# Attention: GpSimd's addition tied to the minimum passes and first in its step, the root's power in two pieces, a third buffer of upper keys, small jobs paired

## The chip, the cores and the metric

The kernel runs on one core of a Trainium2 chip. The time is the device's time of one execution in microseconds; the median of three runs is given with the lowest and the highest. Five engines work side by side, each through its own queue and in the order of that queue: TensorE (PE; its weight loads are listed apart as PEld), VectorE (DVE), ScalarE (ACT), GpSimd (POOL) and SyncE (SP), which here only issues transfers. GpSimd also issues DMAs, among them transfers that add to their destination.

## The reference

A two-layer network on x of 2 x 256 x 64 x 64: an area attention, an LSTM-like recurrence, a Mamba-like convolution block and a mixture of experts, each behind a normalisation and added to its input. The change touches the first block alone:

```python
x = x + _L0_conv_ref(_ln_c(x), ...)
# _ln_c: over the 256 channels, (v - mean) / sqrt(var + 1e-6)
# _L0_conv_ref:
qk = _conv1x1_bn(x, w_qk, ...); vv = _conv1x1_bn(x, w_v, ...)
pp = _bn(depthwise 5x5 convolution of vv)
# 2 images x 4 areas of 1024 positions, 8 heads of 32 channels
attn = softmax(einsum('bhdn,bhdm->bhnm', q, k) * hd ** -0.5)
o = einsum('bhdm,bhnm->bhdn', v, attn)
return _conv1x1_bn(o + pp, w_proj, ...)
```

## The kernel before

**Tiling.** `area_attention` keeps all of x in SBUF, channels on partitions (two blocks c of 128). There are 8 areas of 1024 positions, and in each two groups of 4 heads (the two channel blocks): 16 groups G, called here the first (c = 0) and the second group of an area. A group has 16 steps t: n = t // 8 is the half of 512 queries, m = t % 8 the block of 128 keys. The loop runs over 256 steps.

**A step.** `scores` (L381, L386) makes two PSUM pairs of 2 x 512 scores for four heads, the row maxima (bf16 parts `mx`) being subtracted by a first small matmul; ScalarE takes two exponentials (L393) of them. `values` (L399) multiplies the exponentials of the step before with the transposed values. `maxima` (L286) works one group ahead, for the softmax's row maxima: in even steps with the key difference `kd` (upper minus lower keys), after which ScalarE rectifies both tiles (L298); in odd steps with the lower keys, after which VectorE runs four minimum passes (L302), one a head, that reduce to `nm`. Scores and maxima take four tiles a step from a pool of three pairs (`ps`, six PSUM banks); one more bank `po` serves all other matmuls, one after another, and `av_o` the values.

**Sums of exponentials.** The exponentials of four steps m, m+1, m+2, m+3 are added into the first one's tiles (`sx`, halves 0 and 1): by adding DMAs that GpSimd issues (L596, L602), and in the fourth step by one addition on GpSimd itself (L598), of the third step's half 1, which waits for the last matmul of that step's `maxima`. Three steps later `sums` multiplies them with ones; for the second half of the keys VectorE then runs a chain of five instructions (L425 to L433). In a first group's step 2 this chain belongs to the group before.

**Work for later, by hand.** All else is placed by tables: for each step t a list (offset, function, arguments). The offset counts groups in `BEFORE`, `BEHIND`, `LATE` and areas in `BEHIND_AREA`, `LATE_AREA` (a pair: first group, second group). BEFORE stands between `values` and `maxima`, BEHIND after them, LATE at the end of the step; taps stand ahead of BEHIND in even steps, and in odd steps behind it and `sums`; their number a step is in `TAPS`. The schedule is manual: every engine runs its instructions in the order in which this loop writes them. The functions are:

- next area's normalisation: `mean_sum` (VectorE), `mean_of_sum` (PE, copied by ScalarE), `centre` (VectorE, into the single buffer `xn`, which queries and keys of the area before read until the last query), `square` (ScalarE), `square_sum` (VectorE, L187), `variance_of_sum` (PE, ScalarE), `root` (DVE transpose, GpSimd's add and power, DVE transpose back), `scale` (VectorE);
- `query`, `key`, `v_half`: a projection of 512 columns (L160, four matmuls) that ScalarE evicts; `v_half` with half = 0 also copies border rows on GpSimd; `v_tokens`: four transposes (L249), copied by ScalarE;
- `join`, `place`: row maxima cut into three bf16 parts on GpSimd, turned by TensorE, copied by ScalarE (`rows`) and sent to `mx` by SyncE's DMAs;
- `key_difference` (VectorE, L274), late in step 15; the first matmuls of the next group's step 0 maxima read it;
- the area before: `add_taps`, `output` (L160, then L369 on VectorE), `shift` (ScalarE, L374).

**Taps.** The 5x5 convolution is 50 VectorE instructions an area (L345, L356), handed out by `TAPS`.

The first group has tables of its own (`..._FIRST`): it makes its own row maxima too, two `maxima` in each of its first eight steps.

Of the kernel before, what the change touches and what calls it, by code (L numbers as in the profile page):

```python
# [93 lines left out]
def area_attention(tc, sh, ap):  # L94
# [13 lines left out]
    with ExitStack() as ctx:  # L108
# [29 lines left out]
        early = [None]  # L138

# [17 lines left out]
        def project(wt, c, src, half, out):  # L157

            for k in range(2):
                nc.tensor.matmul(  # L160
                    out, wt[:, k, c * P : (c + 1) * P], src(k)[:, HALVES[half]], start=k == 0, stop=k == 1
                )
# [17 lines left out]
        def mean_sum(A):  # L180
            nc.vector.tensor_tensor(temp("pm", A), area(A)[:, 0], area(A)[:, 1], ALU.add)
# [4 lines left out]
        def square_sum(A):  # L186
            nc.vector.tensor_tensor(temp("sq0", A), temp("sq0", A), temp("sq1", A), ALU.add)  # L187
# [4 lines left out]
        def centre(A, c, at=FULL):  # L192
            if A not in xns:
                xns[A] = p1.tile([P, 2, NA], F32, name="xn")
            nc.vector.tensor_tensor(xns[A][:, c, at], area(A)[:, c, at], temp("pm", A)[:, at], ALU.subtract)
# [7 lines left out]
        def root(A, part, at=FULL):  # L203
            n = (at.stop - at.start) // 32
            if part == 0:
                turned = temp("ln_t", A)[:, at]
                nc.vector.transpose(turned, temp("var", A)[:, at])
                held["turned", at.start] = turned.rearrange("p (k i) -> p k i", i=32)[:, :, 0]
            elif part == 1:
                t = held.pop(("turned", at.start))  # L210
                y = held["root", at.start] = p1.tile([P, NA // 32], F32, name="root")[:, :n]
                nc.gpsimd.tensor_scalar(y, t, 1e-6, None, ALU.add)
                nc.gpsimd.tensor_tensor(y, y, minus_half.to_broadcast([P, n]), ALU.pow)
            else:
                y = held.pop(("root", at.start))
                nc.vector.transpose(
                    temp("ln_r", A)[:, at].rearrange("p (k i) -> p k i", i=32),
                    y.unsqueeze(2).to_broadcast([P, n, 32]),
                )

        def scale(A, c, at=FULL):
            nc.vector.tensor_tensor(xns[A][:, c, at], xns[A][:, c, at], temp("ln_r", A)[:, at], ALU.mult)
# [4 lines left out]
        def v_half(A, c, half):  # L227

            if A not in vhs:
                vhs[A] = p2.tile([P, 2, AROWS + 4, WW], F32, name="vh")  # L230
            ps, r0 = bank(), 2 + half * AROWS // NQ
            project(w["wv"], c, columns(xns[A]), half, ps)
            nc.scalar.activation(
                vhs[A][:, c, r0 : r0 + AROWS // NQ].rearrange("p r w -> p (r w)"), ps, AF.Identity,
                scale=s_v[:, c : c + 1], bias=t_v[:, c : c + 1],
            )
            if half == 0 and AREAS[A][1] > 0:
                nc.gpsimd.tensor_copy(vhs[A][:, c, 0:2], vhs[A - 1][:, c, AROWS : AROWS + 2])
                nc.gpsimd.tensor_copy(vhs[A - 1][:, c, AROWS + 2 :], vhs[A][:, c, 2:4])
# [12 lines left out]
        def rows_of(wt, G, half, name, s, t, ps):  # L252
            A, c = GROUPS[G]
            ps = bank() if ps is None else ps
            project(wt, c, columns(xns[A]), half, ps)
            out = p2.tile([P, 512], F32, name=f"{name}{half}")
            nc.scalar.activation(out, ps, AF.Identity, scale=s[:, c : c + 1], bias=t[:, c : c + 1])
            return out

        def query(G, half, ps=None):  # L260
            if half == 0:
                nms[G] = p2.tile([P, NQ, GH, NM], F32, name="nm")
            qs[G, half] = rows_of(w["wq"], G, half, "q", s_qk, t_qk, ps)

        def key(G, half, ps=None):
            ks[G, half] = rows_of(w["wk"], G, half, "k", s_qk[:, 2:4], t_qk[:, 2:4], ps)
# [4 lines left out]
        def key_difference(G):  # L271

            kds[G] = p1.tile([P, 512], F32, name="kd")
            nc.vector.tensor_tensor(kds[G], ks[G, 1], ks[G, 0], ALU.subtract)  # L274
# [5 lines left out]
        def maxima(G, at):  # L280

            i, n = CHUNKS[at] if G == 0 else divmod(at, 2)
            keys = ks[G, n] if G == 0 else ks[G, 0] if n else kds[G]
            tiles = [wide(), wide()]
            for h in range(GH):
                mm = nc.tensor.matmul(  # L286
                    tiles[h // 2][:, h % 2], qs[G, i // HM][head(h), i % HM * P : (i % HM + 1) * P],
                    keys[head(h)], start=True, stop=True, tile_position=(HD * h, 0),
                )
            if G == 0:  # L290
                for j in range(2):
                    nc.vector.tensor_reduce(  # L292
                        nms[G][:, n, 2 * j : 2 * j + 2, i], tiles[j], AX.X, ALU.max, negate=True
                    )
            elif n == 0:
                held["more"] = [p1.tile([P, 2, 512], F32, name=f"more{j}") for j in range(2)]
                for j in range(2):
                    nc.scalar.activation(held["more"][j], tiles[j], AF.Relu)  # L298
            else:
                for h in range(GH):  # L300
                    more = held["more"][h // 2][:, h % 2]
                    nc.vector.tensor_tensor_reduce(  # L302
                        more, tiles[h // 2][:, h % 2], more, -1.0, 3.0e38, ALU.add, ALU.min,
                        accum_out=nms[G][:, 0, h, i : i + 1],
                    )
            return mm.ins
# [15 lines left out]
        def place(G, half):  # L322
# [8 lines left out]
            mxs[G, half] = p2.tile([P, 512], BF16, name=f"mx{half}")  # L331
# [6 lines left out]
        def taps(A):  # L338

            vh, a = vhs[A], AREAS[A][1]  # L340
            for lower in range(2):
                for c in range(2):
                    if not lower:
                        acc = accs[A, c] = p1.tile([P, AROWS, WW], F32, name=f"acc{c}")
                        nc.vector.tensor_scalar(  # L345
                            acc, vh[:, c, 2 : 2 + AROWS], w_pe[:, c, 12:13], t_pe[:, c : c + 1], ALU.mult, ALU.add
                        )
                        yield
                    for k in range(25):
# [6 lines left out]
                        nc.vector.scalar_tensor_tensor(  # L356
                            part, vh[:, c, 2 + r0 + dy : 2 + r1 + dy, w0 + dx : w1 + dx],
                            w_pe[:, c, k : k + 1], part, ALU.mult, ALU.add,
                        )
                        yield  # L360

        def add_taps(A, c):
            y = ys[A, c]
            nc.vector.tensor_tensor(y, y, accs.pop((A, c)).rearrange("p r w -> p (r w)"), ALU.add)

        def output(A, co, half):
            ps, to = bank(), area(A)[:, co, HALVES[half]]
            project(w["wpr"], co, lambda k: ys[A, k], half, ps)
            nc.vector.scalar_tensor_tensor(to, ps, s_pr[:, co : co + 1], to, ALU.mult, ALU.add)  # L369
# [44 lines left out]
        def sums(G, n, half, exs):  # L414
# [18 lines left out]
            nc.vector.tensor_tensor(y, y, total, ALU.mult)  # L433
# [3 lines left out]
        with ExitStack() as own:  # L437
# [12 lines left out]
            def norm(at, half):  # L450
# [7 lines left out]
                root(0, 1, at)  # L458
                yield
                root(0, 2, at)  # L460
# [13 lines left out]
            query(0, 0, wide()[:, 0])  # L474
# [28 lines left out]
            for c in range(2):  # L503
# [8 lines left out]
        BEFORE = {3: [(0, place, 1)], 14: [(1, place, 0)]}  # L512
        BEHIND = [
            {0: [(1, query, 1)], 11: [(2, query, 0)], 13: [(2, key, 0)], 15: [(2, key, 1)]},
            {5: [(1, query, 1)], 9: [(2, query, 0)], 13: [(2, key, 0)], 15: [(2, key, 1)]},
# [3 lines left out]
                1: [(0, v_tokens, 0, 1), (-1, shift, 0)], 3: [(0, v_tokens, 1, 0), (1, square_sum)],  # L519
                4: [(1, variance_of_sum, 0)], 5: [(1, variance_of_sum, 1), (-1, shift, 1)], 7: [(-1, output, 0, 0)],  # L520
                8: [(-1, output, 0, 1)], 9: [(-1, output, 1, 0)], 12: [(0, v_tokens, 1, 1)],
            },
            {
                0: [(1, v_half, 0, 0)], 1: [(1, v_half, 1, 0)], 3: [(1, v_half, 0, 1), (2, mean_sum)],
                4: [(2, mean_of_sum, 0)], 7: [(-1, output, 1, 1)], 8: [(2, mean_of_sum, 1)],
                11: [(1, v_half, 1, 1)], 12: [(1, v_tokens, 0, 0)],
# [5 lines left out]
                0: [(1, centre, 0)], 1: [(1, centre, 1), (1, square, 0)], 2: [(1, square, 1)],  # L532
                4: [(-1, add_taps, 1)], 6: [(1, root, 0)], 7: [(1, root, 1)],
                9: [(1, root, 2), (1, scale, 0), (1, scale, 1)],
# [5 lines left out]
        BEHIND_FIRST = {**BEHIND[0], 0: [(1, key, 1)]}  # L540
# [6 lines left out]
        for t in range(16):  # L547
# [3 lines left out]
            [2, 0, 1, 1, 2, 2, 2, 1, 2, 0, 0, 2, 3, 2, 3, 0],  # L551
            [4, 1, 1, 1, 3, 2, 3, 2, 2, 1, 1, 2, 2, 1, 2, 0],
# [19 lines left out]
        for g in range(16 * len(GROUPS)):  # L572
# [14 lines left out]
            works(G, t, BEFORE_FIRST if new else BEFORE, {})  # L587

            mm = None
# [5 lines left out]
            if m % 4:  # L595
                nc.gpsimd.dma_start(total[0], exs[0], accum_op=ALU.add)  # L596
# [4 lines left out]
            if m % 2:  # L601
                nc.gpsimd.dma_start(total[1], exs[1], accum_op=ALU.add)  # L602
# [4 lines left out]
            works(G, t, BEHIND_FIRST if new else BEHIND[c], BEHIND_AREA[c])  # L607
# [1724 lines left out]
```

## Time and profile before

| What | us |
|---|---|
| median of 3 runs (lowest, highest) | 2896.4 (2896.26, 2899.74) |
| profiled execution, time | 2893.63 |
| profiled execution, span | 2891.8 |
| attention's loop, from the first score matmul (61.0) to the start of the last group (1293.0) | 1232 |
| areas 1 to 6 of it, 241.2 to 1212.8 | 971.6 |
| TensorE busy in these | 950.80 |
| VectorE, ScalarE, GpSimd busy in these | 836.36, 680.91, 459.06 |

A line of instructions by time reads: start, duration, engine, line, operation, out<-in, shapes, count, and in brackets the idle time of that engine before it and what ended it. A line by stretches reads: from:to, length, then busy time and number of instructions of TensorE, its weight loads, VectorE, ScalarE and GpSimd, the granted TensorE clock (1.00 is full), the mean busy share of the DMA engines and their GB/s. Some instructions of before:

| Instruction | mean ns |
|---|---|
| L393 exponential, L298 rectified maxima (128 x 1024) | 1029 |
| L302 minimum pass, and its read-out | 687, 83 |
| L274 key difference: lowest, median, highest of 15 | 685, 961, 3324 |
| L187 sum of squares: lowest, median, highest of 7 | 1398, 2240, 4094 |
| L598 GpSimd's addition (128 x 1024) | 2684 |
| L213 GpSimd's power, 32 columns; 16 columns | 6359; 2934 |
| L195 centring, L222 scale (128 x 1024) | 1226, 1222 |
| L198 square, L374 shift (128 x 1024) | 1066, 1152 |
| L257 eviction of a query or key, L421 and L412 copies (128 x 512) | 778, 593 |

### The profile page before, as it was taken

What the parts mean: (1) busy time and instruction counts of PE and PEld (TensorE: products, weight loads), DVE (VectorE), ACT (ScalarE), POOL (GpSimd) and SP (SyncE); (2) the same over time, 40 slices, a digit from 0 to 9 for tenths busy, and PEclk for the clock granted to TensorE, in tenths of its full rate; (3) what the DMA queues carried; (4) which work ended last, traced back from release to release, by engine and by line L of the source; (5) the groups of instructions that cost most, each with busy time, mean ns of one, the idle gap of its engine ahead of it and who ended that gap; (6) DMA issues with size and microseconds to landing.
All of it is one profiled execution on the core that took longest, in us unless ns stands there. A gap on an engine that the chain in (4) does not pass through costs nothing.

```text
span 2891.8 us, 45886 instructions
## 1 busy us (share of the span) xinstructions
PE 2631.5 (91%) x17234; PEld 1483.3 (51%) x17234; DVE 1963.8 (68%) x3729; ACT 1554.5 (54%) x2641; POOL 1239.8 (43%) x1164
## 2 busy tenths in 40 slices
PE   7899999999999999997799999878885699999984
PEld 2223333333333333321699999833443588888873
DVE  5788879898888979786566667788887522222116
ACT  3567676666767676763344555576645522222223
POOL 1444545444444445443221000078771266666651
PEclk9999999999999999998899999989998899999995
DMA  3566666666676666767240000035553266666648
GB/s 132 110 128 126 129 128 131 126 132 131 128 137 132 132 132 127 138 130 144 90 175 1 2 1 1 9 99 150 142 136 122 87 235 221 229 225 227 229 171 342
DMA packets 104826, 388.16 MB, mean 134 GB/s; under 512 B 19656, under 2 KB 20560, under 8 KB 94864
## 3 DMA queue, kind: packets, MB, share of 16 engines
q0 software_dynamic: 71488, 293.00, 43.0%
q1 hardware_dynamic: 31872, 87.86, 9.4%
q10 hardware_dynamic: 1232, 4.25, 0.4%
q8 instruction: 138, 2.26, 0.3%
q14 instruction: 96, 0.79, 0.1%
HBM read 173.30 MB, written 43.58 MB: 75 GB/s over the span
## 4 chain that ended last, share of the span: by engine, by line
PE 73%; DVE 11%; issue 5%; DMA 4%; ACT 3%; POOL 3%; SPq 0%; ACTq 0%; DVEq 0%; POOLq 0%
PE ps L286 9%; PE ph L2078 9%; PE py L2088 8%; PE po L160 7%; PE av_o L399 7%; PE z L805 7%; PE z L817 7%; PE ps L386 6%; DMA sx<-ex 3%; PE ps L381 3%; PE yp L1560 2%; PE po L399 2%; DVE hs L1550 2%; DVE more L302 1%; DVE acc L356 1%
## 5 line engine op out<-in xcount | busy, mean ns | idle before, releaser
L356 DVE SCALAR_TENSOR_TENSOR acc<-vh,w_pe,acc 128x1008 f32<-128x1008 f32 (+7 forms) x384 | 529.5, 1382 | 9.1
L596 POOL DMA_DIRECT2D sx<-ex x192 | 166.7, 868 | 692.7 <-DMA sx<-ex 278.3
L393 ACT ACTIVATE ex<-ps 128x1024 f32<-128x1024 f32 x384 | 376.1, 1029 | 125.9 <-PE ps L386 50.4
L302 DVE CUSTOM_DVE_ANT_0 more<-ps,more 128x512 f32<-128x512 f32 x480 | 302.9, 687 | 133.5 <-PE ps L286 124.6
L2080 ACT ACTIVATE act<-ph,wt 128x256 f32<-128x256 f32 x272 | 128.8, 474 | 386.5 <-PE ph L2078 379.1
L2068 DVE COPY xt<-px 128x512 f32<-128x512 f32 x68 | 47.0, 692 | 396.5 <-PE px L2066 396.5
L2078 PE MATMUL ph<-xt,wt 128*128 128x256 f32 x1088 | 291.6, 391 | 5.0 <-ACT act L2080 3.0
L386 PE MATMUL ps<-q,k 32*128 32x512 f32 x2048 | 285.2, 602 | 0.0
L2088 PE MATMUL py<-wt,act 128*128 128x256 f32 x1088 | 278.7, 379 | 0.0
L298 ACT ACTIVATE more<-ps 128x1024 f32<-128x1024 f32 x240 | 233.4, 1028 | 26.8 <-issue 9.1
L2078 PEld LDWEIGHTS ph<-xt,wt 128*128 128x128 f32 x1088 | 190.4, 191 | 68.0 <-DVE xt L2068 24.0
L805 PE MATMUL z<-xs,u 128*128 128x128 f32 x1872 | 224.0, 277 | 0.0
L805 PEld LDWEIGHTS z<-xs,u 128*128 128x128 f32 x1872 | 217.7, 194 | 0.2 <-issue 0.2
L829 ACT ACTIVATE t<-z,bias 128x128 f32<-128x128 f32 x468 | 136.3, 361 | 145.1 <-PE z L817 145.1
L399 PE MATMUL av_o<-ex,vt 128*32 128x512 f32 x1536 | 212.0, 613 | 2.4 <-ACT ex L393 2.4
L2088 PEld LDWEIGHTS py<-wt,act 128*128 128x128 f32 x1088 | 201.6, 190 | 24.7
L2103 POOL DMA_INDIRECT results<-y,ri x136 | 138.0, 1014 | 138.9 <-DVE y L2096 115.6
L286 PE MATMUL ps<-k,q 32*128 32x512 f32 x1088 | 182.6, 639 | 1.7 <-DVE nm L292 1.3
L817 PE MATMUL z<-xs,v 128*128 128x128 f32 x1512 | 180.0, 275 | 0.1
L817 PEld LDWEIGHTS z<-xs,v 128*128 128x128 f32 x1512 | 174.2, 192 | 0.7 <-DVE xs L836 0.7
L598 POOL TENSOR_TENSOR sx<-sx,ex 128x1024 f32<-128x1024 f32 x64 | 171.8, 2684 | 4.7 <-PE ps L286 4.7
L1557 POOL TENSOR_TENSOR cs<-hs,cs 128x1024 f32<-128x1024 f32 x63 | 149.0, 2367 | 55.4 <-DVE hs L1550 33.8
(435 smaller groups left out, 4607.8 us busy)
## 6 DMA issues: line engine op xcount, KB each, us to landing
sx<-ex POOLq DMA_DIRECT2D x320, 512.0 KB
cs<-c_rows SPq DMA_DIRECT2D x128, 256.0 KB
y<-results SPq DMA_DIRECT2D x32, 512.0 KB
x<-xrows SPq DMA_DIRECT2D x8, 1024.0 KB
rows<-xt SPq DMA_DIRECT2D x16, 512.0 KB
out_x<-res POOLq DMA_DIRECT2D x15, 512.0 KB
xrows<-xn SPq DMA_DIRECT2D x24, 256.0 KB
x<-in_x SPq DMA_DIRECT2D x4, 1024.0 KB
```

What stands on the lines that cost most here:

```text
L160: nc.tensor.matmul(out, wt[:, k, c * P : (c + 1) * P], src(k)[:, HALVES[half]], start=k == 0, stop=k == 1)
L286: mm = nc.tensor.matmul(tiles[h // 2][:, h % 2], qs[G, i // HM][head(h), i % HM * P : (i % HM + 1) * P], keys[head(h)], start=True, stop=T ...
L298: nc.scalar.activation(held["more"][j], tiles[j], AF.Relu)
L302: nc.vector.tensor_tensor_reduce(more, tiles[h // 2][:, h % 2], more, -1.0, 3.0e38, ALU.add, ALU.min, accum_out=nms[G][:, 0, h, i : i + 1],)
L356: nc.vector.scalar_tensor_tensor(part, vh[:, c, 2 + r0 + dy : 2 + r1 + dy, w0 + dx : w1 + dx], w_pe[:, c, k : k + 1], part, ALU.mult, ALU.add,
L386: nc.tensor.matmul(tiles[h // 2][:, h % 2], k[head(h), m % HM * P : (m % HM + 1) * P], qs[G, n][head(h)], start=False, stop=True, tile_pos ...
L393: nc.scalar.activation(exs[i], tiles[i], AF.Exp, scale=HD**-0.5)
L399: nc.tensor.matmul(to[head(h)], lhs, exs[h // 2][:, h % 2], start=first, stop=last, tile_position=(0, HD * h))
L805: nc.tensor.matmul(z[c][:, g, :m], u[:, k, c, g], xt[:, k], start=g == GATES[0] and k == 0, stop=False, skip_group_check=True,)
L817: nc.tensor.matmul(z[c][:, g, :m], v[:, k, c, g], h[:, k], start=False, stop=k == 1, skip_group_check=True,)
L2078: nc.tensor.matmul(ph[:, hc], wt[:, at : at + P], xt[:, c], start=c == 0, stop=c == 1)
L2088: nc.tensor.matmul(py[:, j], act[:, hc, j * P : j * P + P], wt[:, at : at + C], start=hc == 0, stop=hc == NH - 1,)
```

## The change

- **Addition.** In the fourth step of four, GpSimd's addition (L598) now stands ahead of both DMAs of that step, not between them. It waits for the second matmul that `maxima` writes, not the last, and besides for the VectorE instruction that was written last before this step's `maxima` (`mark` notes the instructions that count).
- **Root.** `root` has four parts: the add and the power on GpSimd come in two pieces of half the columns; in the tables the pieces stand in steps 6 and 7, the transpose in step 5, the transpose back and the first scale in step 8.
- **Buffers.** `k1` gets three buffers; `mx0` and `mx1` one each.
- **Jobs.** `query` and `output` can be called for 256 columns. The tables are written anew: keys come ahead of queries, halved projections stand in even steps, two small jobs share an odd step (one ahead of the maxima, in `BEFORE` or the new `BEFORE_AREA`, one behind). Both centrings move one step later; the squares stay in steps 1 and 2.

```diff
-            elif part == 1:
-                t = held.pop(("turned", at.start))
-                y = held["root", at.start] = p1.tile([P, NA // 32], F32, name="root")[:, :n]
-                nc.gpsimd.tensor_scalar(y, t, 1e-6, None, ALU.add)
-                nc.gpsimd.tensor_tensor(y, y, minus_half.to_broadcast([P, n]), ALU.pow)
-            else:
+                held["root", at.start] = p1.tile([P, NA // 32], F32, name="root")[:, :n]
+            elif part == 3:
                 y = held.pop(("root", at.start))
...
+            else:
+                cut = slice((part - 1) * n // 2, part * n // 2)
+                y, t = held["root", at.start][:, cut], held["turned", at.start][:, cut]
+                nc.gpsimd.tensor_scalar(y, t, 1e-6, None, ALU.add)
+                nc.gpsimd.tensor_tensor(y, y, minus_half.to_broadcast([P, n // 2]), ALU.pow)
...
+    def columns_of(half, part):
+        return HALVES[half] if part is None else slice(512 * half + 256 * part, 512 * half + 256 * part + 256)
...
+            ks[G, half] = p2.tile([P, 512], F32, name=f"k{half}", bufs=2 + half)
...
-            return mm.ins
+            return made[1].ins
...
-            mxs[G, half] = p2.tile([P, 512], BF16, name=f"mx{half}")
+            mxs[G, half] = p1.tile([P, 512], BF16, name=f"mx{half}")
...
-        BEFORE = {3: [(0, place, 1)], 14: [(1, place, 0)]}
+        BEFORE = {2: [(0, place, 1)], 14: [(1, place, 0)]}
+        BEFORE_AREA = [
+            {3: [(0, v_tokens, 1, 0)], 4: [(0, v_tokens, 0, 1)], 5: [(1, variance_of_sum, 0)]},
+            {15: [(2, mean_of_sum, 0)]},
+        ]
         BEHIND = [
-            {0: [(1, query, 1)], 11: [(2, query, 0)], 13: [(2, key, 0)], 15: [(2, key, 1)]},
-            {5: [(1, query, 1)], 9: [(2, query, 0)], 13: [(2, key, 0)], 15: [(2, key, 1)]},
+            {1: [(1, query, 1)], 11: [(2, key, 1)], 13: [(2, key, 0)], 15: [(2, query, 0)]},
+            {
+                0: [(1, query, 1, 0)], 4: [(1, query, 1, 1)], 8: [(2, query, 0, 0)], 9: [(2, key, 1)],
+                12: [(2, query, 0, 1)], 13: [(2, key, 0)],
+            },
         ]
         BEHIND_AREA = [
             {
-                1: [(0, v_tokens, 0, 1), (-1, shift, 0)], 3: [(0, v_tokens, 1, 0), (1, square_sum)],
-                4: [(1, variance_of_sum, 0)], 5: [(1, variance_of_sum, 1), (-1, shift, 1)], 7: [(-1, output, 0, 0)],
-                8: [(-1, output, 0, 1)], 9: [(-1, output, 1, 0)], 12: [(0, v_tokens, 1, 1)],
+                0: [(1, mean_of_sum, 1), (-1, shift, 0)], 3: [(0, v_tokens, 1, 1), (1, square_sum)],
+                4: [(-1, shift, 1)], 5: [(1, variance_of_sum, 1)], 7: [(-1, output, 0, 0)],
+                8: [(-1, output, 1, 0, 0)], 9: [(-1, output, 0, 1)], 12: [(-1, output, 1, 0, 1)],
             },
             {
-                0: [(1, v_half, 0, 0)], 1: [(1, v_half, 1, 0)], 3: [(1, v_half, 0, 1), (2, mean_sum)],
-                4: [(2, mean_of_sum, 0)], 7: [(-1, output, 1, 1)], 8: [(2, mean_of_sum, 1)],
-                11: [(1, v_half, 1, 1)], 12: [(1, v_tokens, 0, 0)],
+                1: [(1, v_half, 0, 0)], 3: [(1, v_half, 1, 0), (2, mean_sum)], 5: [(-1, output, 1, 1)],
+                7: [(1, v_half, 0, 1)], 11: [(1, v_half, 1, 1)], 15: [(1, v_tokens, 0, 0)],
             },
         ]
         LATE = {11: [(1, join, 0)], 15: [(2, key_difference), (1, join, 1)]}
         LATE_AREA = [
             {
-                0: [(1, centre, 0)], 1: [(1, centre, 1), (1, square, 0)], 2: [(1, square, 1)],
-                4: [(-1, add_taps, 1)], 6: [(1, root, 0)], 7: [(1, root, 1)],
-                9: [(1, root, 2), (1, scale, 0), (1, scale, 1)],
+                1: [(1, centre, 0), (1, square, 0)], 2: [(1, centre, 1), (1, square, 1)],
+                4: [(-1, add_taps, 1)], 5: [(1, root, 0)], 6: [(1, root, 1)], 7: [(1, root, 2)],
+                8: [(1, root, 3), (1, scale, 0)], 9: [(1, scale, 1)],
             },
...
         TAPS = [
-            [2, 0, 1, 1, 2, 2, 2, 1, 2, 0, 0, 2, 3, 2, 3, 0],
-            [4, 1, 1, 1, 3, 2, 3, 2, 2, 1, 1, 2, 2, 1, 2, 0],
+            [2, 0, 0, 0, 2, 0, 3, 1, 1, 0, 1, 2, 2, 2, 3, 0],
+            [4, 1, 1, 1, 3, 2, 2, 2, 3, 1, 1, 2, 3, 2, 3, 0],
         ]
...
-            mm = None
+            mm, last_op = None, latest[0]
...
-            if m % 4:
-                nc.gpsimd.dma_start(total[0], exs[0], accum_op=ALU.add)
             if m % 4 == 3:
                 add = nc.gpsimd.tensor_tensor(total[1], total[1], pending[3][1], ALU.add)
                 if mm is not None:
                     tc.add_manual_dep(add.ins, mm.name, at_end, reason="beside the reductions")
-            if m % 2:
-                nc.gpsimd.dma_start(total[1], exs[1], accum_op=ALU.add)
+                    tc.add_manual_dep(add.ins, last_op.name, at_end, reason="beside the reductions")
+            for i in ((), (0, 1), (0,), (0, 1))[m % 4]:
+                nc.gpsimd.dma_start(total[i], exs[i], accum_op=ALU.add)
```

## The prediction

> **What bounds the kernel now.** I read the page's engine shares first, then busy time by stretches, cut at the starts of the six middle areas (1 to 6), then the timeline.
>
> ```profile
> PE 2631.5 (91%) x17234; PEld 1483.3 (51%) x17234; DVE 1963.8 (68%) x3729; ACT 1554.5 (54%) x2641; POOL 1239.8 (43%) x1164
> ...
> 241.20:406.10 164.90, 159.83 (x1058) 50.12 (x1053) 138.85 (x217) 113.66 (x133) 77.69 (x71) 0.99 0.68 128
> 406.10:568.10 162.00, 158.85 (x1056) 49.83 (x1052) 141.95 (x215) 113.67 (x133) 74.79 (x70) 1.00 0.69 130
> ...
> 1053.20:1212.80 159.60, 156.60 (x1056) 49.52 (x1056) 139.30 (x214) 112.73 (x131) 76.41 (x71) 1.00 0.70 132
> sum 971.60, PE 950.80 PEld 298.89 DVE 836.36 ACT 680.91 POOL 459.06; mean PE 158.47 PEld 49.82 DVE 139.39 ACT 113.49 POOL 76.51
> ```
>
> TensorE is busy 950.8 of 971.6 us: an area costs its matmuls, and what it waits is all that a reordering can win. From the starts of the scores, a step with a job of about 1.06 us (sums, mean, variance) lasts 4.48 us, one with a 1.98 us projection 5.40, one with four transposes 4.26 unless it waits; so 3.42 goes without a job. Where the longer waits come from is seen at a boundary, and, in the first group of an area, at steps 2 and 3 (step 3 starts at 908.00):
>
> ```profile
> 324.96 3.32 DVE L274 TENSOR_TENSOR kd<-k,k 128x512 f32<-128x512 f32 x1 [0.22 <-ACT k L257]
> 325.04 2.69 POOL L598 TENSOR_TENSOR sx<-sx,ex 128x1024 f32<-128x1024 f32 x1
> ...
> 328.34 1.14 PE L286 MATMUL ps<-kd,q 32*128 32x512 f32 x8 [1.99 <-DVE kd L274]
> ```
>
> ```profile
> 905.94 0.30 PEld L286 LDWEIGHTS ps<-kd,q 32*128 32x128 f32 x4 [0.36 <-ACT ex L393]
> ...
> 908.13 0.69 DVE L425 TENSOR_TENSOR sum<-sum,po 128x512 f32<-128x512 f32 x1 [1.55 <-PE po L399]
> ...
> 908.49 1.08 ACT L198 ACTIVATE sq<-xn 128x1024 f32<-128x1024 f32 x1
> ...
> 909.44 1.96 ACT L393 ACTIVATE ex<-ps 128x1024 f32<-128x1024 f32 x2
> ...
> 910.63 0.69 DVE L433 TENSOR_TENSOR y<-y,sum 128x512 f32<-128x512 f32 x1
> ```
>
> The key difference takes 3.32 us beside GpSimd's addition against 0.69 at the fastest, and TensorE waits 1.99 us. The second fence has two things to keep: half of the maxima (L286) cannot start before the first exponential of its own step is done (three PSUM pairs for four tiles), and VectorE is held from 908.13 to 911.32 by the chain of the sums. ScalarE's second square of the area (908.49) got in ahead of the exponentials only because its centring had run one step earlier.
>
> **The addition tied to the minimum passes.** Four passes run 2.5 us (687 ns each, overlapped by read-outs of 83 ns), the addition 2.69. Beside one another they fit, and the key difference and the sum of squares (4.09 us at worst, 1.40 at best) should be free of it. The waits this removes lie inside the 971.6. The addition now stands ahead of both DMAs of its step, so the first is issued some 3 us later; the pair lands 4.5 and 7 us after its issue and is needed three steps (some 14 us) after its step, so I cost that at nothing. In the last group, where 36.1 us of GpSimd's waits are for its own DMAs, an addition that no longer stands behind such a wait wins up to 1.9 us in each of four quads: -5 in all (0 to -8).
>
> **Root in two pieces.** 32 columns took 1.27 + 6.36 us on GpSimd, 16 took 0.28 + 2.93. Two pieces go into steps 6 and 7, but the second is queued behind addition and DMAs of step 7 and ends about 2.2 us into step 9; the DVE transpose (1.24) and scale (1.22) behind it then hold the minimum passes of step 9 by 1.3 us, and with a 1.98 us job ahead of the next scores 0.5 us of that reaches TensorE. The early roots gain a second instruction: +0.4 at the start.
>
> **Third upper-key buffer, keys before queries.** The key difference no longer waits for the eviction of a key in step 15. This costs nothing (the 2 KB come from the second buffers of the row maxima, whose readers end at least two steps before the next write). Between the first areas two taps still stand ahead of it at a boundary: with taps of 1.25 us I keep 1.6 us of wait there, once in group 1 and once in group 2.
>
> **Small jobs paired.** Odd steps get long jobs or two short ones, even steps one short. Summed without other waits: the first group's steps 0 to 5 are 4.48 + 5.40 + 4.55 + 5.45 + 4.26 + 5.84 = 29.98 (0.35 and 0.30 of wait kept in steps 3 and 5, as rows of such steps show), steps 6 to 15 50.03 with the 0.5 from the root, the second group 79.41. Halved projections are counted at 1.06 us, four matmuls of 256 columns at about 0.27 (291.6 us for 1088 on L2078). So 159.4 us an area against 161.9 now: -15 in six areas, were that all.
>
> **What is moved with it is not free.** Centring of channel 0 moves from step 0 to 1, of channel 1 from step 1 to 2, but their squares stay in steps 1 and 2. Each square now stands in ScalarE's queue directly behind a centring that VectorE has yet to do, and ahead of the next step's exponentials. Walked from the start of a first group with durations of rows above:
> - Step 0: exponentials to 3.3, copy of y 0.6, rectified maxima (L298) to 5.6, copy of the mean 0.6, shift 1.15: ScalarE is free at 7.2, and step 1's exponentials, ready at 5.8, start there. The second half of step 1's maxima waits; the query's projection ends at 11.2 where 9.9 was due.
> - Step 1: centring waits for that query (its buffer is single), to 12.5; square to 13.6; exponentials of step 2 start 1 us late; the row copy of the new place stands behind them and holds the sums' bank. Step 3 starts at 16.9 instead of 14.4.
> - Step 2 to 3: the sums' chain holds VectorE 3.3 us into step 3, centring to 4.5, square to 5.6 (ScalarE idle meanwhile), exponentials 5.6 to 7.5 instead of 1.4 to 3.4. Half of step 3's maxima waits from 3.9 for the first of them (6.6); the second transposes' bank waits until the copy behind both is done (8.15). Step 3 lasts 8.85, not 5.45.
> - Steps 4 and 5: copy, rectified maxima and shift overfill ScalarE, and the second variance waits for the first one's copy: 10.95, not 10.10.
>
> So steps 0 to 5 take 4.45 + 6.75 + 5.65 + 8.85 + 10.95 = 36.65, 6.7 more than 29.98. An area is 166.1, six are 996.6: **+25.0** against 971.6. Nothing covers it, since TensorE has no other work released.
>
> The half-rate clock comes on top. Two of the waits now were followed by a window of 0.50:
>
> ```profile
> 160.18:163.59 3.41, 1.17 (x9) 0.41 (x9) 3.34 (x5) 1.16 (x2) 3.18 (x5) 1.00 0.74 139
> 163.59:167.01 3.42, 3.42 (x4) 1.00 (x4) 1.03 (x1) 1.94 (x2) 1.34 (x2) 0.50 0.13 24
> 324.02:327.43 3.41, 2.34 (x21) 0.65 (x20) 3.19 (x5) 2.86 (x4) 2.96 (x2) 1.00 0.50 96
> 242.10:245.51 3.41, 1.31 (x16) 0.35 (x16) 3.38 (x4) 2.42 (x3) 2.96 (x5) 1.00 0.84 159
> 245.51:248.93 3.42, 3.42 (x10) 1.02 (x8) 3.02 (x3) 1.61 (x2) 1.18 (x2) 0.50 0.32 60
> ```
>
> Idle stretches of 2.54 and 2.10 us that fell into one window cost 1.6 us each (a 1.98 us projection took 3.68); the 1.99 us split between two windows cost none. The wait of some 2.7 us in step 3 lies with 2.1 or more in one window in about 6 of 10 phases: 6 x 0.6 x 1.6 = **+5.6**; ends 0 and 6 x 3.4 (two windows each) = 20. I take the middle, as gaps of 2.10 and 2.54 both fell on that side.
>
> The Trainium skill ("TensorE: Matmul & The Clock Gate", The HAM clock gate) lets the clock fall only after a whole idle window of about 3.4 us. By that rule the 5.6 would be 0 and the total 5.6 us lower; the rows above show it falling after windows with 1.17 and 1.31 us of work, so the sum does not use the rule.
>
> **Sum**, against the profiled execution (2893.6 us, span 2891.8): areas 1 to 6 +25.0; clock +5.6; taps ahead of the key difference in group 2 +1.6; group 0, where squares also stand behind centrings while VectorE takes 4.6 us of reductions a step, +3 (0 to 5); group 1 from 83.3 to 81.0, -2.3; group 14 -1; last group -5; start +0.4: +27.3, so 2920.9. The median of the runs is 2.8 us above this execution; I put the time at 2921, between.
>
> **Rivals.**
> - *The waits in ScalarE's queue are covered (faster).* For it: the -15 of paired jobs, -2.3, -1, -5 stand. Against: the 0.36 us wait for an exponential above shows that half of the maxima do stop. Price without it: -15 + 1.6 - 2.3 - 6 + 0.4 = -21, 2872 to 2875. It decides if the delays cost under 3.5 us an area, half of my 6.7. Chance 0.14.
> - *The clock falls at every delay, for two windows.* For it: steps 3 to 5 hold several waits in a row. Against: they hold matmuls between. +20 in place of 5.6: 2936. Chance 0.09.
> - *The tie does not hold the addition beside the passes* (the change doesn't do what it says): in step 3 it waits for the marked centring, and DMAs behind it come late, as 19.1 us of ScalarE's waits for a buffer in the last group show can happen. The contention stays: about the 1.99 + 1.54 + 1.24 + 1.02 + 0.95 + 1.85 = 8.6 of waits now, and up to 8 us of late DMAs: 2930 to 2938. Chance 0.07.
>
> **How the numbers follow.** My forecast has 0.70, with its own range 2907 to 2935 (delays of 4.5 to 7.5 us an area, clock 0 to 10). The range over all, 2886 to 2938, leaves out most of the first rival and the tail of the second. A measurement tells 0.2% (5.8 us) from no change. Faster is the first rival, 0.14; within the bound a tail of my own delays, 0.04; slower the rest, 0.82.
>
> **What would show it.** Right: in first groups of areas 1 to 6 step 3 lasts near 9 us; ScalarE's square there is idle before it for VectorE's centring, 3 us or more; half-rate windows follow some of them; the key difference stays under 1.1 us; GpSimd's power takes two times 3 us. Wrong: exponentials of step 3 start 1.4 us after the step, or step 3 lasts under 6 us, or steps 0 to 5 take under 32 us. The forecast fails most easily if buffering lets TensorE run on where I stop it.

## The result and the profile after

The changed kernel takes 2927.1 us (median of 4 runs, 2922.3 to 2930.7) against 2897.1 for the kernel before on the same chip: 1.0101 times as long, 95% interval 1.0083 to 1.0118. The profiled execution took 2922.3 us (span 2920.0), 28.6 more than that of before. The forecast was 2921, the range 2886 to 2938, slower with a chance of 0.82.

Busy time by stretches, changed kernel, cut at the starts of areas 1 to 6 (columns as before):

```profile
243.10:414.20 171.10, 164.24 (x1068) 52.61 (x1067) 131.69 (x218) 114.44 (x134) 80.45 (x73) 0.97 0.66 124
414.20:581.90 167.70, 163.24 (x1064) 52.40 (x1064) 129.36 (x216) 114.01 (x134) 79.76 (x73) 0.98 0.67 126
...
1083.40:1250.00 166.60, 162.50 (x1066) 52.41 (x1065) 128.17 (x215) 113.43 (x133) 79.71 (x73) 0.98 0.67 127
sum 1006.90, PE 976.97 PEld 313.42 DVE 773.67 ACT 684.10 POOL 473.16; mean PE 162.83 PEld 52.24 DVE 128.94 ACT 114.02 POOL 78.86
```

The six areas take 1006.9 us instead of 971.6, while VectorE is busy 62.7 us less: what GpSimd's addition had slowed now runs at its own speed, the key difference at 0.69 us and the sum of squares at 1.22 (0.69 to 3.32 and 1.40 to 4.09 before):

```profile
L287 DVE TENSOR_TENSOR kd<-k,k x15: 684/686/691, 70.8 to 1251.1; 128x512 f32<-128x512 f32 x15
L196 DVE TENSOR_TENSOR sq<-sq,sq x7: 1214/1220/1221, 94.6 to 1109.8; 128x1024 f32<-128x1024 f32 x7
```

TensorE's busy time, matmuls at half rate included, grew by 26.2 us. The steps of a first group, mean of areas 1 to 6, from the first score matmul of each to the next:

| us | 0 | 1 | 2 | 3 | 4 | 5 | 0 to 5 | 6 to 15 | second group |
|---|---|---|---|---|---|---|---|---|---|
| before | 6.33 | 4.61 | 5.11 | 4.78 | 5.12 | 4.77 | 30.7 | 50.6 | 80.7 |
| predicted | 4.45 | 6.75 | 5.65 | 8.85 | 10.95 for both | | 36.65 | 50.0 | 79.4 |
| after | 5.14 | 6.39 | 5.57 | 9.24 | 6.12 | 5.88 | 38.3 | 50.0 | 79.4 |

Steps 2 and 3 of a first group after the change, from the timeline (area 5; step 2 starts at 927.5, step 3 at 933.0):

```profile
932.94 0.69 DVE L439 TENSOR_TENSOR sum<-sum,po 128x512 f32<-128x512 f32 x1 [4.25 <-PE po L413]
...
935.44 0.69 DVE L447 TENSOR_TENSOR y<-y,sum 128x512 f32<-128x512 f32 x1
935.57 0.30 PEld L299 LDWEIGHTS ps<-k,q 32*128 32x128 f32 x4 [0.17 <-issue]
935.57 1.13 PE L299 MATMUL ps<-k,q 32*128 32x512 f32 x4
936.05 1.22 DVE L204 TENSOR_TENSOR xn<-x,pm 128x1024 f32<-128x1024 f32 x1
...
937.30 1.06 ACT L207 ACTIVATE sq<-xn 128x1024 f32<-128x1024 f32 x1 [3.73 <-DVE xn L204]
...
938.26 1.92 ACT L407 ACTIVATE ex<-ps 128x1024 f32<-128x1024 f32 x2
...
939.32 1.13 PE L299 MATMUL ps<-k,q 32*128 32x512 f32 x4 [2.62 <-ACT ex L407]
```

This is the chain of the prediction, link by link: the centring starts at 936.05, as the sums' chain (L439 to L447) ends, the square at 937.30 after ScalarE stood idle for 3.73 us, and only behind it come the exponentials (L407), at 938.26, 5.2 us into the step (1.4 before). Half of the maxima (L299, four of eight) waits 2.62 us for the first of them. In areas 3 to 5 one stretch of 3.41 us at half the clock follows this wait, in areas 1, 2 and 6 two in a row; such stretches are called half-rate windows below. Over the whole kernel the squares account for it so (the line's waits, changed kernel):

```profile
L207 ACT ACTIVATE sq<-xn x18: 617/1057/1058, 12.9 to 1104.3; 128x1024 f32<-128x1024 f32 x14, 128x512 f32<-128x512 f32 x4
...
  DVE xn L204: 38.0, 14
```

ScalarE waited 38.0 us for VectorE's centring ahead of 14 squares; in the kernel before, the same view lists no idle time of ScalarE ahead of its squares.

### The profile page after: what moved, and what is told of

It reads as the page before. It is cut to its first block, busy times and chain, and to the rows that moved or that the text cites. A ratio compares the mean times of both kernels' runs of the same rounds, so it can differ in the third digit from the quotient of the medians.

```text
span 2920.0 us, 46186 instructions
## 1 busy us (share of the span) xinstructions
PE 2653.3 (91%) x17318; PEld 1496.6 (51%) x17318; DVE 1887.6 (65%) x3736; ACT 1557.5 (53%) x2655; POOL 1255.9 (43%) x1182
## 4 chain that ended last, share of the span: by engine, by line
PE 76%; DVE 10%; issue 5%; DMA 3%; ACT 2%; POOL 2%; SPq 0%; ACTq 0%; DVEq 0%; POOLq 0%
PE ps L299 10%; PE ph L2099 9%; PE av_o L413 8%; PE py L2109 8%; PE po L169 7%; PE ps L400 7%; PE z L826 7%; PE z L838 7%; PE ps L395 3%; PE po L413 2%; PE yp L1581 2%; DVE hs L1571 2%; DMA sx<-ex 2%; PE px L2087 1%; PE po L181 1%
## 5 line engine op out<-in xcount | busy, mean ns | idle before, releaser
L369 DVE SCALAR_TENSOR_TENSOR acc<-vh,w_pe,acc 128x1008 f32<-128x1008 f32 (+7 forms) x384 | 482.5, 1258 | 9.3
L623 POOL DMA_DIRECT2D sx<-ex x320 | 281.0, 959 | 464.5 <-ACT ex L407 338.2
L407 ACT ACTIVATE ex<-ps 128x1024 f32<-128x1024 f32 x384 | 373.7, 1026 | 129.2 <-issue 60.0
L400 PE MATMUL ps<-q,k 32*128 32x512 f32 x2048 | 291.9, 612 | 0.0
L618 POOL TENSOR_TENSOR sx<-sx,ex 128x1024 f32<-128x1024 f32 x64 | 152.7, 2385 | 265.0 <-PE ps L299 215.4
L299 PE MATMUL ps<-k,q 32*128 32x512 f32 x1088 | 195.4, 651 | 17.7 <-ACT ex L407 16.1
```

What stands on the lines that cost most here:

```text
L299: made.append(nc.tensor.matmul(tiles[h // 2][:, h % 2], qs[G, i // HM][head(h), i % HM * P : (i % HM + 1) * P], keys[head(h)], start=True, ...
L369: mark(nc.vector.scalar_tensor_tensor(part, vh[:, c, 2 + r0 + dy : 2 + r1 + dy, w0 + dx : w1 + dx], w_pe[:, c, k : k + 1], part, ALU.mult, ...
L400: nc.tensor.matmul(tiles[h // 2][:, h % 2], k[head(h), m % HM * P : (m % HM + 1) * P], qs[G, n][head(h)], start=False, stop=True, tile_pos ...
L407: nc.scalar.activation(exs[i], tiles[i], AF.Exp, scale=HD**-0.5)
L623: nc.gpsimd.dma_start(total[i], exs[i], accum_op=ALU.add)
```

## The experiments

Each kernel was timed beside the kernel before on the same chip. That kernel took 2901.8 us in the first set, 2900.9 and 2900.8 in the others, so kernels are compared by their ratios to it.

**The squares one step later.**

```diff
# in the changed kernel
-                3: [(0, v_tokens, 1, 1), (1, square_sum)],
-                4: [(-1, shift, 1)], ...
+                3: [(0, v_tokens, 1, 1)],
+                4: [(1, square_sum), (-1, shift, 1)], ...
...
-                1: [(1, centre, 0), (1, square, 0)], 2: [(1, centre, 1), (1, square, 1)],
+                1: [(1, centre, 0)], 2: [(1, centre, 1), (1, square, 0)], 3: [(1, square, 1)],
```

> The changed kernel with its two squares one step later, so that in ScalarE's queue each stands a whole step behind its centring (square of channel 0 at the end of step 2, of channel 1 at the end of step 3, the sum of squares in step 4). Nothing else differs. Theory (ScalarE's exponentials are held by squares that wait for VectorE's centring): in first groups of areas 1 to 6 step 3 falls from 8.7-9.75 us to about 5.5, step 2 from 5.5 to 4.8, and with them the half-rate clock windows there; 5 to 6 us an area and some 4 in the first group, so 2885 to 2895 us against 2927. Rival (the new job tables overfill the first steps whatever the squares wait for): steps 0 to 5 keep at least 35 of their 37.4-38.2 us, 2912 us or more.

Measured: 2892.8 us, ratio 0.9972 (0.9962 to 0.9983), against 1.0101 with the squares joined. Step 3 fell to 5.52 us in all six areas, step 2 to 4.48, steps 0 to 5 to 32.5, the areas to 971.7. Half-rate time in the areas fell from 34.1 us (ten windows: nine behind step 3's wait, one in step 0 of area 1) to 3.4. From the timeline of area 5 (step 3 starts at 909.4):

```profile
910.11 1.06 ACT L207 ACTIVATE sq<-xn 128x1024 f32<-128x1024 f32 x1
...
911.05 1.94 ACT L407 ACTIVATE ex<-ps 128x1024 f32<-128x1024 f32 x2
...
912.12 1.14 PE L299 MATMUL ps<-k,q 32*128 32x512 f32 x8
912.44 1.22 DVE L204 TENSOR_TENSOR xn<-x,pm 128x1024 f32<-128x1024 f32 x1
```

The square of channel 0 has nothing to wait for, the exponentials start 1.6 us into the step, and all eight matmuls of the maxima run in one piece. The centring of channel 1 is as late as ever, but nothing of ScalarE stands behind it. That is the theory's side, and more than the whole loss.

**That one line alone, in the kernel before.**

```diff
# in the kernel before
-                0: [(1, centre, 0)], 1: [(1, centre, 1), (1, square, 0)], 2: [(1, square, 1)],
+                1: [(1, centre, 0), (1, square, 0)], 2: [(1, centre, 1), (1, square, 1)],
```

> The kernel before, with one line of the change alone: both centrings one step later, so that each square follows its own centring in the same step. Theory: the exponentials of step 3 start 5 to 6 us after the step instead of 1.4, steps 0 to 5 of first groups grow by 5 to 7 us in areas 1 to 6, half-rate windows follow: 2930 to 2950 us against 2897. Rival (the loss comes from the split projections, the tie or the paired jobs): within 6 us of 2897.

Measured: 2947.7 us, ratio 1.0159 (1.0130 to 1.0189). Steps 0 to 5 grew by 6.7 us to 37.4, the areas from 971.6 to 1013.7. Its timeline in area 5 (step 3 starts at 945.2):

```profile
947.65 0.69 DVE L433 TENSOR_TENSOR y<-y,sum 128x512 f32<-128x512 f32 x1
948.26 1.22 DVE L195 TENSOR_TENSOR xn<-x,pm 128x1024 f32<-128x1024 f32 x1
949.51 1.06 ACT L198 ACTIVATE sq<-xn 128x1024 f32<-128x1024 f32 x1 [3.86 <-DVE xn L195]
950.47 1.92 ACT L393 ACTIVATE ex<-ps 128x1024 f32<-128x1024 f32 x2
...
951.53 2.08 PE L286 MATMUL ps<-k,q 32*128 32x512 f32 x4 [3.04 <-ACT ex L393]
```

The same four links with much the same waits (3.86 and 3.04 us, against 3.73 and 2.62), without any paired job, tie or split root. The last line runs at half rate: four matmuls took 2.08 us instead of 1.13.

**The addition's part alone.**

```diff
# in the kernel before: mark() as in the change, and
-            if m % 4:
-                nc.gpsimd.dma_start(total[0], exs[0], accum_op=ALU.add)
             if m % 4 == 3:
                 add = nc.gpsimd.tensor_tensor(total[1], total[1], pending[3][1], ALU.add)
...
+                    tc.add_manual_dep(add.ins, last_op.name, at_end, ...)
-            if m % 2:
-                nc.gpsimd.dma_start(total[1], exs[1], accum_op=ALU.add)
+            for i in ((), (0, 1), (0,), (0, 1))[m % 4]:
+                nc.gpsimd.dma_start(total[i], exs[i], accum_op=ALU.add)
...
-            return mm.ins
+            return made[1].ins
```

> The kernel before, with the addition's part of the change alone (first in its step, tied to the second matmul of the maxima and to the VectorE instruction before). Theory: the key difference stays under 1.1 us and the sum of squares under 1.5; the waits of 1.99, 1.54, 1.24, 1.02, 0.95 and 1.85 us go (-8.6), the two boundaries with half-rate windows win some 4 us, the last group some 5: 2875 to 2885 us against 2897. Rival (the addition's wait holds up the DMAs queued behind it on GpSimd, and the exponentials that need their buffers): 2897 or more.

Measured: 2875.9 us, ratio 0.9906 (0.9885 to 0.9926). The areas fell to 957.3 us, with no half-rate time in them. The key difference, lowest, median and highest of 15, in the kernel before and in this one:

```profile
L274 DVE TENSOR_TENSOR kd<-k,k x15: 685/961/3324, 70.5 to 1213.4; 128x512 f32<-128x512 f32 x15
```

```profile
L279 DVE TENSOR_TENSOR kd<-k,k x15: 682/719/726, 75.4 to 1201.1; 128x512 f32<-128x512 f32 x15
```

So one part of the change wins about 0.9%, and another, alone, loses 1.6%.

**First in its step, without the tie.**

```diff
# in the kernel before: only the order; the addition still waits for the maxima's last matmul
-            if m % 4:
-                nc.gpsimd.dma_start(total[0], exs[0], accum_op=ALU.add)
             if m % 4 == 3:
                 add = ...
-            if m % 2:
-                nc.gpsimd.dma_start(total[1], exs[1], accum_op=ALU.add)
+            for i in ((), (0, 1), (0,), (0, 1))[m % 4]:
+                nc.gpsimd.dma_start(total[i], exs[i], accum_op=ALU.add)
```

> The kernel before with the addition first in its step, but waiting for the last matmul of the maxima as before and for no VectorE instruction. Theory (what made it late was the DMA ahead of it in GpSimd's queue): nearly all of the gain of the addition's part, areas 1 to 6 within 3 us of its 957.3, key difference under 1.1 us. Rival (the tie does it): areas 965 us or more, key difference still above 2 us in places.

Measured: 2875.2 us, ratio 0.9916 (0.9892 to 0.9939); areas 957.3, key difference at most 0.693 us. The boundary that had cost 1.99 us reads here (timeline; step 0 starts at 322.3):

```profile
320.42 2.35 POOL L596 TENSOR_TENSOR sx<-sx,ex 128x1024 f32<-128x1024 f32 x1 [4.44 <-PE ps L286]
322.72 1.76 POOL L600 DMA_DIRECT2D sx<-ex  x2
323.03 0.69 DVE L274 TENSOR_TENSOR kd<-k,k 128x512 f32<-128x512 f32 x1 [0.22 <-ACT k L257]
```

The tie to a matmul was there before. What had made the addition late was the DMA issue ahead of it in GpSimd's queue, which waited 4.76 us for the DMA before; in the kernel before, the same boundary (step 0 starts at 324.3) reads:

```profile
324.47 0.86 POOL L596 DMA_DIRECT2D sx<-ex  x1 [4.76 <-DMA sx<-ex]
325.04 2.69 POOL L598 TENSOR_TENSOR sx<-sx,ex 128x1024 f32<-128x1024 f32 x1
```

The two new waits add nothing that these runs can tell.

**The shifts moved out of ScalarE's full steps.**

```diff
# in the changed kernel
-                0: [(1, mean_of_sum, 1), (-1, shift, 0)], ...
-                4: [(-1, shift, 1)], 5: [(1, variance_of_sum, 1)], 7: [(-1, output, 0, 0)],
+                0: [(1, mean_of_sum, 1)], ...
+                5: [(1, variance_of_sum, 1), (-1, shift, 0)], 7: [(-1, output, 0, 0), (-1, shift, 1)],
```

> The changed kernel with the two shifts of the area before (1.15 us each on ScalarE) moved from steps 0 and 4 to steps 5 and 7; the squares stay joined to their centrings. Theory: step 1 falls from 6.5 to about 5.6 and steps 4 and 5 together from 12.0 to about 11, but step 3 keeps 8 us or more, since there it is VectorE's chain that holds the square: 2912 to 2920 us. Rival (ScalarE's load in the first steps is the cause): step 3 falls below 6.5 us, 2900 or less.

Measured: 2927.8 us, ratio 1.0095 (1.0069 to 1.0121): no gain, where 7 to 15 us were expected. Step 1 fell to 5.52 as expected, but step 2 rose to 5.94 and step 3 to 9.75, and half-rate time from 34.1 to 44.4 us, since all six areas now have two windows behind step 3's wait; steps 4 and 5 kept 11.94. Steps 0 to 5 are 38.3, as before the edit. Step 3 stays far over 6.5, which speaks against load on ScalarE as the cause; my price for taking the load away was wrong.

**All that was found, mended.** The squares and shifts as above, and:

```diff
-                8: [(1, root, 3), (1, scale, 0)], 9: [(1, scale, 1)],
+                9: [(1, root, 3), (1, scale, 0), (1, scale, 1)],
...
-            [2, 1, 2, 2, 2, 2, 2, 2, 2, 1, 2, 2, 2, 2, 2, 2],
+            [4, 1, 2, 2, 2, 2, 2, 2, 2, 1, 2, 2, 2, 2, 2, 0],
```

> The changed kernel with the squares one step later (as in the run above), both shifts in steps 5 and 7, the transpose back of the root and both scales in step 9, and the two taps of step 15 that stand ahead of the key difference of group 2 moved to step 0. Theory (with these mended, the paired jobs cost their 159.4 us an area): steps 0 to 5 of first groups 30.0 to 30.5 us, areas 1 to 6 together 955 to 962 us, the whole about 0.8 to 0.9% below the kernel before, the same as the addition's part alone (areas 957.3): the paired jobs then bring nothing of their own. Rival (the pairing wins once nothing is in its way): 948 us or less in areas 1 to 6.

Measured: 2884.2 us, ratio 0.9944 (0.9925 to 0.9962); areas 963.5, a little over the expected 955 to 962, and 6 us over the addition alone. Steps 0 to 5 are 31.0: step 4 keeps 5.06 where 4.26 was due, since its transposes stand ahead of the maxima and nothing is left behind them to cover the rectified maxima that the next scores need. Step 9 fell to 5.43, but step 11 rose to 5.82. Against the addition alone the areas gain 0.6 us each in steps 6 to 15 and the second group (129.5 for 130.1) and lose 1.6 in steps 0 to 5 (31.0 for 29.4). So the new tables as a whole win nothing even with these obstacles gone; the root's two pieces and the buffers, which this kernel also has, were not timed apart.

**Taps moved away from two key differences**, on top of the addition's part.

```diff
-            [0, 0, 0, 0, 1, 1, 1, 1, 1, 1, 2, 2, 3, 2, 3, 2],
-            [2, 1, 2, 2, 2, 2, 2, 2, 2, 1, 2, 2, 2, 2, 2, 2],
+            [0, 0, 0, 0, 1, 1, 1, 1, 1, 1, 2, 2, 3, 2, 3, 0],
+            [4, 2, 2, 2, 2, 2, 2, 2, 2, 2, 2, 2, 2, 2, 2, 0],
```

> The addition's part alone, and besides the taps of step 15 in areas 0 moved to earlier and later steps, so that no tap stands ahead of the key differences of groups 1 and 2. Theory: step 0 of groups 1 and 2 falls from 6.6 and 6.8 us to 5.4, 2 to 3 us in all, 2872 to 2874 us if the run of the addition's part is 2876. Rival: two taps more in the steps before hold other waits, no gain.

Measured: 2877.0 us, ratio 0.9917 (0.9893 to 0.9941). Step 0 of groups 1 and 2 fell from 6.58 and 6.81 to 5.35 each, 2.7 us, but the runs can't tell the whole from the run without it. The three runs with the addition's part (by itself, as a mere change of order, and with these taps) can't be told from one another; each beats both kernels.

**Work inside the wait, first try.** What the half-rate clock costs can't be read from a step's length alone, so TensorE was given work inside step 3's wait.

```diff
# in the changed kernel, for step 3 of the first groups of areas 1 to 7: again = 3
-            for h in range(GH):
+            for h in [0, 1] * again + [2, 3]:
```

> The changed kernel, but in step 3 of the first groups the maxima's matmuls of heads 0 and 1 are issued three times over with the same result, so that TensorE has some 2.1 us of work inside its wait of 2.6 us for the exponential; the wait itself stays. Theory (part of the loss is the half-rate clock after that wait): half-rate windows in areas 1 to 6 fall from 34 us to 10 or less, steps 0 to 5 from 38.3 to about 36.7 us, the areas together from 1006.9 to about 998. Rival (the clock costs nothing, since the steps behind it wait for ScalarE anyway): steps 0 to 5 stay within 0.4 us of 38.3.

Measured: 2929.1 us, ratio 1.0104 (1.0077 to 1.0131). Half-rate time fell only to 23.9 us, steps 0 to 5 to 37.9, the areas to 1004.0. In areas 1 to 5 the clock still fell, though TensorE's idle time in step 3 had shrunk to 0.91 us. In area 6 it stayed full, with the square and the exponentials as late as in the changed kernel (step 3 starts at 1104.6); the two stretches are steps 0 to 5 of area 6, here and in the changed kernel:

```profile
1108.88 1.06 ACT L207 ACTIVATE sq<-xn 128x1024 f32<-128x1024 f32 x1 [3.73 <-DVE xn L204]
1109.84 1.92 ACT L407 ACTIVATE ex<-ps 128x1024 f32<-128x1024 f32 x2
...
1110.90 1.13 PE L299 MATMUL ps<-k,q 32*128 32x512 f32 x4 [0.91 <-ACT ex L407]
```

```profile
1088.00:1123.85 35.85, 33.56 (x211) 10.39 (x211) 21.69 (x40) 25.30 (x31) 13.29 (x15) 1.00 0.59 112
1083.40:1121.48 38.08, 34.33 (x203) 10.42 (x202) 21.60 (x40) 25.30 (x31) 13.28 (x15) 0.91 0.56 106
```

So the same delays cost 35.85 us at full clock and 38.08 with two half-rate windows; areas 2 to 5 of this run, with one window each, took 37.4. One window cost 1.6 us, which is the theory's figure (38.3 to 36.7), and the rival, for which the clock costs nothing, is out.

**Second try, with full matmuls.**

```diff
+            for k in range(warm):    # 2 in step 3 of those groups
+                nc.tensor.matmul(tiles[0][:, k % 2], w["wq"][:, 0, :P], qs[G, 0], start=True, stop=True)
             for h in range(GH):
```

> The changed kernel, but in step 3 of the first groups two matmuls of 512 columns on all 128 rows (1.98 us, their result overwritten by the maxima that follow) stand ahead of the maxima, inside what is TensorE's wait for the exponential. In the run with repeated half-row matmuls the clock still fell after windows with 2.25 to 2.50 of 3.41 us of work. Theory (matmuls on two of four row strips count for less): half-rate windows in areas 1 to 6 fall below 10 us, steps 0 to 5 to about 36.7 us, the areas to about 997 us against 1006.9, which prices the clock at 9 to 10 us. Rival (any wait of this kind brings the clock down): half-rate windows stay above 20 us.

Measured: 2928.8 us, ratio 1.0097 (1.0076 to 1.0117); half-rate time 20.5 us, areas 1003.0, steps 0 to 5 37.7. By the letter this is the rival's side: a window with little waiting is enough. In area 5, the window in which the wait lies, and the one after it:

```profile
939.92:943.33 3.41, 2.24 (x14) 0.73 (x11) 2.01 (x7) 2.76 (x4) 2.74 (x2) 1.00 0.00 0
943.33:946.74 3.41, 3.41 (x21) 0.85 (x20) 3.38 (x5) 1.64 (x3) 1.32 (x2) 0.50 0.79 148
```

In area 1 of this run no window followed step 3's wait, and steps 0 to 5 took 38.73 us, against 41.52 with two such windows in the changed kernel. With area 6 of the first try this prices the clock in the changed kernel: 2.8 us in area 1, 2.3 in area 2, 1.6 in each of areas 3 to 5 and 2.2 in area 6 are 12.1 us of the 1006.9, for the nine windows behind step 3's wait.

## Why the prediction was right

- **What bounds it**: right. Areas cost TensorE's work plus its waits; with VectorE busy 62.7 us less they still grew by 35.3.
- **Squares behind centrings**: right, and shown from both sides, by mending it in the changed kernel (1.0101 to 0.9972) and by bringing it alone into the kernel before (1.0159). The walk gave 36.65 us for steps 0 to 5 without the clock, and 35.85 were measured at full clock (area 6 of the first try), by steps 4.60, 6.52, 5.51, 8.49 and 10.73 for the walk's 4.45, 6.75, 5.65, 8.85 and 10.95. So the walk has every link and is 0.8 us an area too long, 4.8 in six.
- **Half-rate clock**: right in kind and in the price of a window, mis-sized in their number. The term was +5.6 (6 x 0.6 x 1.6 is 5.8): 3.6 windows of 1.6 us. One window did cost 1.6, but nine followed step 3's wait, at least one in every area, and together they cost 12.1. The Trainium skill ("TensorE: Matmul & The Clock Gate", The HAM clock gate) gives half rate as the state after at least one idle window of about 3.4 us. By that rule the term would have been nothing; here the measurement differs, since the window of the second try shown above, with 2.24 of 3.41 us of work in it, was followed by half rate.
- **Addition**: its mechanism was right. The key difference is at most 0.691 us after the change, and the last group, from its first score matmul to its last step's, won 4.5 us, for -5. That its DMAs come later cost nothing seen. Giving the tie a part in it was wrong: in the kernel before, the order alone gave the whole gain.
- **Paired jobs**: the -15 that I set beside them, "were that all", was the addition's. The addition's part by itself brought the areas to 957.3 us, within 1 us of the 6 x 159.4 = 956.4 that I had put down to both together; the new tables add nothing to that and, mended, still cost 6 us. The 29.98 for steps 0 to 5 lacked the 0.8 us at the end of step 4, which only the walk had.
- **Root in two pieces**: +0.5 expected in step 9, 5.78 us against 5.40, so about 0.4; but in five of areas 1 to 6 the two powers took 3.7 and 3.9 us, not the 2.93 that was counted for each. The loop starts 0.4 us later, as said.
- **Group 0**: +3 predicted, +4.6 measured. Steps 2 and 3 grew by 3.0, of which 2.5 went when the squares moved; the rest is in steps 5 and 9 to 11 and was not looked into. Groups 1 and 14 and the last won 3.1, 2.1 and 4.5, for 2.3, 1 and 5.

The sum was +27.3 against the profiled execution, which grew by 28.6. The size is partly luck. Areas 1 to 6 were put at +32.2: 25.0 for the delays, 5.6 for the clock and 1.6 for the wait in group 2. They came to +35.3: 20.3 for the delays, 12.1 for the clock, and 2.9 by which steps 0 to 5 of area 1 (its first group is group 2) are longer than those of other areas without the windows behind step 3's wait. So delays that were put too high covered much of a clock that was put too low; and what stands behind the loop ran 2.4 us shorter, which no term had.

## What to carry to other kernels

In a queue that runs in order, look at what each moved instruction waits for, and at what stands behind it: here two squares of 1 us, placed one step too close to their source on another engine, held the exponentials and with them TensorE, and cost more than all the rest of the change won. Before tying an instruction to others with new waits, look at what stands ahead of it in its own queue: moving one DMA issue behind the addition gave all of the gain. When a change has several parts, time them apart; this one held a part that gains 0.9% under a total that loses 1.0%.

## What the runs showed of the hardware

The clock fell after windows of 3.41 us in which TensorE's recorded work filled 2.24 to 2.50 us, when part of it was matmuls on two of four row strips (the first try), and when two full matmuls stood ahead (the second, 2.24 to 2.25). In the kernel before, a window with 2.34 us of work kept the full clock, and in the kernel before with joined squares windows with 1.90 and 2.17 did too; the first of them and the window behind it:

```profile
591.84:595.25 3.41, 1.90 (x10) 0.80 (x11) 3.37 (x3) 1.72 (x3) 2.96 (x5) 1.00 0.80 151
595.25:598.66 3.41, 3.41 (x25) 0.91 (x25) 1.33 (x2) 3.23 (x5) 1.37 (x2) 1.00 0.54 101
```

The share of recorded busy time alone does not decide it; what does stays open.

A single half-rate window behind step 3's wait cost 1.6 us. A second one directly behind it cost 0.7 in areas 2 and 6 and 1.2 in area 1 of the changed kernel; TensorE worked 5.73 of the two windows' 6.83 us in area 2, and 6.71 of 6.82 in area 1.
